# Three reorderings in a selective-scan kernel: the loads at its head, the spread of C behind dt, and attention steps beside the last slots of the layers

## The chip, the cores and the metric

The kernel runs on one core of a Trainium2 chip. The metric is device time in microseconds (us) of the whole program, lower is better. A core has a matrix engine (PE), a vector engine (DVE), an activation engine (ACT), a general engine (POOL) and a queue engine (SP) that in this kernel issues nearly all DMAs. Each of them runs its own list of instructions in the order of the program and waits on semaphores for the others.

## The reference, cut to what matters

The input `x` is two images of 128 channels and 64x64 pixels. Four layers follow. The first (`_L0`) is a 1x1 embedding, two blocks of a Mamba mixer and a feed-forward, and a 1x1 output with a residual. The mixer is where most of the first two thousand microseconds go:

```python
xz = x @ in_w.T; u, z = split(xz)                    # 128 -> 2 x 256 channels
u = silu(causal_conv(u, conv_w, 4 taps) + conv_b)
dt, Bm, Cm = split(u @ xproj_w.T, [8, 8 + 16])       # per pixel: 8, 16 and 16 numbers
dt = softplus(dt @ dt_w.T + dt_b)                    # 256 channels
dA = exp(dt[..., None] * A);  dBu = (dt * u)[..., None] * Bm[:, :, None, :]
h = dA_t * h + dBu_t;  y_t = einsum('bdn,bn->bd', h, C_t)     # over 4096 pixels
y = (y + u * ssm_D) * silu(z);  return y @ out_w.T
```

The second layer (`_L1`) has queries, keys and values from 3x3 convolutions, softmax attention over all 4096 pixels and a residual. The third (`_L2`) is the same with 1x1 convolutions. The fourth (`_L3`) has convolutions at four scales and a small attention between them. The change touches the first layer and its border with the second.

## The kernel before

**Items and slots.** An item is one chunk of 512 pixels of one block of one image: `items` has 2 images x 2 blocks x 8 chunks = 32 of them. The 256 channels times 16 states of an item are scanned in 8 groups of 32 channels; a group is four scans, each of 128 partitions (32 channels x 4 states) by 512 pixels. So an item has 32 slots of one scan. The body of a slot is `slot(i, todo, t_)`, run for i from -2 to 31 and then for a tail. `background(i)` writes by hand which pieces of the neighbouring items go into which slot (`at(slot, function, ...)`): for the next item n = i+1 the mixer's front, for i-1 and i-2 the mixer's back and the feed-forward, for i+2 the embedding and the layer norm. The schedule is manual: every engine gets its instructions in just this order.

**One item.** `pu_taps` (PE) makes u with the conv folded into the weights `wu`; `pu_out` (ACT) adds the bias; `silu` runs in slot 11; `xproj` in slot 13 and `xproj_out` in slot 14 give dt, B and C. `spread_bc` then stores B and C to a DRAM tile `dr` (1 DMA) and reads them back broadcast over the partitions: B into `bb` with four DMAs of 256 KB, C into `cb` with four more. `soft_plus` (slot 17) and `dt_end` (POOL, slot 18) give dt and dt*u. For each group, `spread_dt` copies dt of 32 channels four times into `dtb` (four DMAs of 64 KB, ring of four buffers, three groups ahead), `spread_dtu` brings dt*u onto 128 partitions with a matmul (`pdu`), `times_b` multiplies it with B into `h` on DVE, `decay` makes `da` = exp(dt*A) on ACT, `scan` runs the recurrence on DVE, and when a group's four scans are done POOL multiplies `h` with C. `y_pair` sums on PE. `ln_centre` to `ln_shift` are the layer norm.

**The head.** SP issues first the constants, then all eight chunks of image 0, then the embedding's weights `we`, then for each of the two blocks `wl`, `cw` (conv taps and the u half of the weights), `wd`, then the raw 3x3 weights `raw` (3 loads) and image 1. DVE multiplies `wu` from `cw`, and a short chain ACT, DVE, PE, DVE makes `am` (A spread over the partitions), for both blocks, before slot 0 of i = -2. In the slots of i = -1, `fold(k)` for k = 0, 1, 2 turns the raw weights into the form the attention's convolutions want (10 DVE operations) and stores them to DRAM as `ufold` (2 DMAs): in slots 2, 10 and 18.

**The tail.** The scans end with i = 31. The slots of i = 32 and 33 finish the last items' mixer and feed-forward (gelu in slot 3, `ffn_down` in slots 6 and 7, `ffn_add` in 9, `out_mm` in 11, `out_add` in 12 of the last round). Beside them a generator `beginning()` makes the first queries and the keys of the attention: `inputs` (12 DVE operations on the image, in two parts of 8 and 4), `products_by` (six groups of matmuls, with a `yield` after each), `outputs` (2 ACT and 9 DVE operations). The digits of

```python
beside = '2111001000112111111011010000'
```

say how many `next(steps)` stand in front of each tail slot, from slot 8 on; what remains runs after the last slot. The generator has 31 yields: 1 for the start, 6 for the queries, 6 for each of four chunks of keys (cc = 0 to 3). After that come the attention's scores, evicted by DVE (`sc`).

Of the kernel before, what the change touches and what calls it, by code (L numbers as in the profile page):

```python
# [6 lines left out]
F32 = mybir.dt.float32  # L7
AF = mybir.ActivationFunctionType
ALU = mybir.AluOpType
# [4 lines left out]
B, C, H, W = 2, 128, 64, 64  # L14
N = H * W
P = 128
CH = 512
NCH = N // CH
RPC = CH // W
NL = 2  # L20
DS = 16
DI = 2 * C
NJ = DI // P
R = (C + 15) // 16
NX = R + 2 * DS
KC = 4
# [41 lines left out]
def tile_conv_seq(ctx: ExitStack, tc, x, consts, vecs, wemb, wlay, wconv, wdt, wqkv, wsmall, wms, out):  # L68
    nc = tc.nc
# [9 lines left out]
    def xv(b, c):  # L79

        return xt[:, b, 1 + c * RPC : 1 + (c + 1) * RPC, 1 : W + 1]
# [7 lines left out]
        nc.gpsimd.memset(xt[:, b, 1 : H + 1, 0:1], 0.0)  # L89
        nc.gpsimd.memset(xt[:, b, 1 : H + 1, W + 1 : W + 2], 0.0)  # L90

    for c in range(NCH):
        nc.sync.dma_start(xv(0, c), x[0, :, c * RPC : (c + 1) * RPC, :])

    ud = ctx.enter_context(tc.tile_pool(name="ufold", bufs=1, space=bass.MemoryType.DRAM))
    ufold = [ud.tile([P, 18, C], F32, name=f"ufold{k}") for k in range(3)]
# [17 lines left out]
    with tc.manual_schedule(), ExitStack() as s:  # L114
# [22 lines left out]
            return fsel[:, g].rearrange("p q d -> p (q d)")  # L137

        nc.scalar.preload_act_table_set(EXP_LN_SET)
        wl, wu, wd, am = [], [], [], []  # L140
        for l in range(NL):
            w = wp.tile([P, NWL - DI], F32, name=f"wl{l}")
            nc.sync.dma_start(w, wlay[l][:, DI:])
            cw = sp.tile([P, KC + 1, DI], F32, name="cw", tag="h", bufs=5)
            nc.sync.dma_start(cw[:, :KC, :].rearrange("p k d -> p (k d)"), wconv[l : l + 1, :].to_broadcast([P, KC * DI]))
            nc.sync.dma_start(cw[:, KC, :], wlay[l][:, :DI])
            d = wp.tile([R, DI], F32, name=f"wd{l}")
            nc.sync.dma_start(d, wdt[l])

            u = wp.tile([P, KC, DI], F32, name=f"wu{l}")  # L150
            for k in range(KC):
                nc.vector.tensor_tensor(u[:, k, :], cw[:, KC, :], cw[:, k, :], ALU.mult)
            an = wp.tile([P, NJ * DS], F32, name=f"an{l}")
            nc.scalar.activation(an, vec[:, VEC[f"A_log{l}"] : VEC[f"A_log{l}"] + NJ * DS], AF.Exp)
            nc.vector.tensor_scalar(an, an, -1.0, None, ALU.mult)
            a = wp.tile([P, NJ, 4, 4], F32, name=f"am{l}")
            for g in range(4):
                pa = mm.tile([P, NJ, DS], F32, name="pa", tag="mm")
                nc.tensor.matmul(pa.rearrange("p j n -> p (j n)"), lhsT=four(g), rhs=an, start=True, stop=True)
                for q in range(4):  # L160
                    at = slice(32 * q, 32 * q + 32)
                    nc.vector.tensor_copy(a[at, :, g, :], pa[at, :, 4 * q : 4 * q + 4])
            wl.append(w), wu.append(u), wd.append(d), am.append(a)
        raws = []
        for which in range(3):
            raw = sp.tile([P, 3, 3, C], F32, name="raw", tag="h", bufs=5)
            nc.sync.dma_start(raw.rearrange("p y x c -> p (y x) c"), wqkv[:, which])
            raws.append(raw)
        for c in range(NCH):
            nc.sync.dma_start(xv(1, c), x[1, :, c * RPC : (c + 1) * RPC, :])  # L170

        def fold(which):

# [150 lines left out]
            st[i]["dbl"] = sp.tile([NX, CH], F32, name="dbl", tag="dbl")  # L324
            nc.scalar.copy(st[i]["dbl"], st[i].pop("pd"))

        def spread_bc(i):

            dr = dp.tile([2 * DS, CH], F32, name="dr", tag="dr")
            nc.sync.dma_start(dr, st[i]["dbl"][R:])  # L330
            for k in range(2):
                o = st[i]["bc", k] = sp.tile([P, 4, CH], F32, name=("bb", "cb")[k], tag=("bb", "cb")[k], bufs=2)
                for q in range(4):
                    src = dr[k * DS + 4 * q : k * DS + 4 * q + 4, :].rearrange("(o m) f -> o (m f)", o=1)
                    nc.sync.dma_start(o[32 * q : 32 * q + 32].rearrange("p m f -> p (m f)"), src.to_broadcast([32, 4 * CH]))

        def dtproj(i, j):
            st[i]["pt", j] = mmt("pt")
# [131 lines left out]
        def background(i):  # L470

            todo = [[] for _ in range(NSL)]

            def at(t, f, *a):
                todo[t].append((f, a))

            n, p, q, r = i + 1, i - 1, i - 2, i + 2
            if has(q):
                at(3, gelu, q)
                at(6, ffn_down, q, (0, 1)), at(7, ffn_down, q, (2, 3)), at(9, ffn_add, q)  # L480
                at(11, out_mm, q), at(12, out_add, q)
            if has(p):
                at(7, y_out, p, 1), at(7, gate, p)
                at(9, mix_out, p), at(11, mix_add, p)
            if has(n):
                at(0, pu_taps, n, 0, (0, 1)), at(1, pu_taps, n, 0, (2, 3)), at(2, pu_out, n, 0)
                at(3, pu_taps, n, 1, (0, 1)), at(4, pu_taps, n, 1, (2, 3)), at(5, pu_out, n, 1)
                at(13, xproj, n), at(14, xproj_out, n), at(14, spread_bc, n)
                at(15, dtproj, n, 0), at(16, dtproj, n, 1), at(17, soft_plus, n), at(18, dt_end, n)
            if has(i):  # L490
                at(1, pz_mm, i, 0), at(3, pz_out, i, 0)
                at(5, pz_mm, i, 1), at(6, pz_out, i, 1)
            if has(i) or has(n):
                at(11, silu, i, n)
            if i == -1:
                for k in range(3):
                    at(8 * k + 2, fold, k)
            pair = [(k, second) for k, second in ((p, True), (r, False)) if has(k)]
            if has(r):
                at(10, embed, r), at(11, embed_out, r)  # L500
            w, m = {}, len(pair)
            for k, (it, second) in enumerate(pair):
                at(12 + 2 * k, ln_centre, w, k, it)
                at(13 + 2 * k, ln_square, w, k, it)
                at(27, ln_spread, w, k, m), at(28, ln_scale, w, k, it)
                at(29, ln_shift, w, k, it, second)
            if pair:
                at(17, ln_var, w, m), at(18, ln_eps, w, m), at(19, ln_rs, w, m), at(20, ln_newton, w, m), at(21, ln_step, w, m)
            if has(p):
                for f in range(4):  # L510
                    at(30 + f // 2, ffn_up, p, f)
            if has(i):
                at(24, y_out, i, 0)
            return todo
# [6 lines left out]
        def slot(i, todo, t_):  # L521
            t = i * NSL + t_
            g, m = divmod(t, 4)
            if m == 0 and 0 <= g + 3 < NG:
                spread_dt(g + 3)
            if m == 0 and 0 <= g + 1 < NG:
                spread_dtu(g + 1)
            if m == 0 and g % 2 == 1 and 0 <= g - 3 < NG:
                y_pair(g - 3)
            if 0 <= t < NT:  # L530
                scan(t)
            if 0 <= t + 4 < NT:
                decay(t + 4)
            if m == 3 and 0 <= g + 1 < NG:
                times_b(g + 1)
            for f, a in todo[t_]:
                f(*a)
# [305 lines left out]


        steps = beginning()
        beside = '2111001000112111111011010000'
        for k in range(8, 2 * NSL):
            if k == NSL:
                todo = background(NI + 1)
# [523 lines left out]
```

## Time and profile before

| | us |
|---|---|
| median of three runs (5076.55 to 5080.12) | 5076.93 |
| the profiled execution | 5077.7 |
| its span, first to last instruction | 5075.9 |
| first scan starts | 84.94 |
| last scans of the layers end | 2102.91 |
| last `out_add` of the layers starts | 2166.28 |
| first eviction of attention scores starts | 2189.13 |
| mean granted PE clock | 0.948 |

Busy over the span: PE 92%, DVE 81%, ACT 47%, POOL 46%. In the profile a line number is that of the kernel before. A line of the timeline gives the start in us, the duration in us, engine, line, operation, what it writes and reads, its shape, how many were merged, and in brackets how long the engine stood idle before it and what ended that idle time. SPq and ACTq are the issuing of a DMA, not its transfer.

### The profile page before, as it was taken

To read this page: it belongs to the slowest core of one execution; us is meant where nothing else is said; L and a number is where in the kernel's file an instruction comes from. 1 tells how busy PE (TensorE), PEld (TensorE's weight loads), DVE (VectorE), ACT (ScalarE), POOL (GpSimd) and SP (SyncE) were. 2 spreads that over 40 slices of the span, in tenths; PEclk is the share of its full clock that TensorE was granted. 3 is DMA by queue.
4 is the path that set the end of the run, shared out by engine and by line. 5 is a ranking of instruction groups with operands and counts; after the bars stand their busy time and mean duration, and the time that the engine had idled before them with its cause. 6 is when DMAs were issued, how large, how long until landed. Compare 5 with 4: busy or idle time off the path is not lost.

```text
span 5075.9 us, 48999 instructions
## 1 busy us (share of the span) xinstructions
PE 4683.8 (92%) x14797; PEld 2250.9 (44%) x14797; DVE 4097.5 (81%) x4416; ACT 2366.9 (47%) x3221; POOL 2316.3 (46%) x1948
## 2 busy tenths in 40 slices
PE   5889999999988899889999999999999999999997
PEld 1222222222222222356666666666666666333332
DVE  5999999999999999788888878667766775667775
ACT  4677777777777777522222222333333332323332
POOL 2777776766777777413332233233333332322331
PEclk8898889988999989899999999999999999999998
DMA  5333333333333333124443344444444443000000
GB/s 149 72 69 68 70 71 70 72 69 68 69 70 68 72 72 71 46 54 102 105 102 84 77 104 103 118 97 111 111 100 99 112 111 77 5 5 7 7 7 7
DMA packets 237016, 373.86 MB, mean 74 GB/s; under 512 B 88000, under 2 KB 88400, under 8 KB 228432
## 3 DMA queue, kind: packets, MB, share of 16 engines
q1 hardware_dynamic: 187600, 303.55, 25.8%
q10 hardware_dynamic: 49152, 67.17, 5.8%
q8 instruction: 118, 1.93, 0.2%
q14 instruction: 146, 1.20, 0.1%
HBM read 92.18 MB, written 9.83 MB: 20 GB/s over the span
## 4 chain that ended last, share of the span: by engine, by line
PE 47%; POOL 21%; DVE 13%; issue 11%; DMA 3%; ACT 3%; SPq 2%; ACTq 0%; DVEq 0%; POOLq 0%
POOL h L391 16%; PE po L775 13%; PE pq L725 13%; DVE tr L755 3%; DMA pt<-tr 2%; PE pf L1060 2%; SPq L766 2%; PE py L403 2%; PE pqkv L1087 2%; PE pu L292 1%; PE pw L1146 1%; POOL dtu L351 1%; PE pfus L1211 1%; POOL z L414 1%; PE psc L1111 1%
## 5 line engine op out<-in xcount | busy, mean ns | idle before, releaser
L762 POOL COPY pt<-tr 32x512 f32<-32x512 f32 x1024 | 656.1, 641 | 1468.2 <-DVE tr L755 738.8
L388 DVE TENSOR_TENSOR_SCAN h<-da,carry,h 128x512 f32<-128x512 f32 x1024 | 1241.4, 1266 | 60.4 <-ACT da L377 31.6
L391 POOL TENSOR_TENSOR h<-h,cb 128x2048 f32<-128x2048 f32 x256 | 1161.1, 4536 | 20.8 <-POOL carry L390 0.2
L725 PE MATMUL pq<-k,q 128*128 128x512 f32 x2048 | 965.1, 594 | 11.2 <-DVE sc L730 8.8
L775 PE MATMUL po<-pt,vt 128*128 128x256 f32 x4096 | 967.5, 380 | 2.4 <-DMA pt<-tr 2.4
L740 ACT ACTIVATE sc<-sc,nm 128x2048 f32<-128x2048 f32 x256 | 510.6, 1995 | 937.2 <-DVE nm L736 641.7
L730 DVE TENSOR_SCALAR_CACHE_REDUCE sc<-pq 128x1024 f32<-128x1024 f32 x512 | 624.9, 1222 | 359.8 <-PE pq L725 337.9
L775 PEld LDWEIGHTS po<-pt,vt 128*128 128x128 f32 x4096 | 780.5, 191 | 293.9 <-issue 211.1
L377 ACT ACTIVATE da<-dtb,am 128x512 f32<-128x512 f32 x1024 | 681.7, 684 | 222.1 <-DVE h L388 210.6
L755 DVE STREAM_TRANSPOSE tr<-sc 128x2048 f32<-128x2048 f32 x256 | 591.6, 2311 | 65.8 <-DMA pt<-tr 60.5
L370 DVE TENSOR_TENSOR h<-bb,pdu 128x2048 f32<-128x2048 f32 x256 | 581.7, 2272 | 77.4 <-PE py L403 29.3
L403 PE MATMUL py<-h,sel 128*32 128x512 f32 x2048 | 511.5, 643 | 1.6 <-POOL h L391 1.6
L725 PEld LDWEIGHTS pq<-k,q 128*128 128x128 f32 x2048 | 384.5, 191 | 289.5 <-issue 247.1
L364 PE MATMUL pdu<-dtu,fsel 128*128 128x512 f32 x512 | 326.5, 724 | 101.9 <-DVE h L370 101.8
L403 PEld LDWEIGHTS py<-h,sel 128*32 128x32 f32 x2048 | 115.7, 118 | 415.9 <-issue 408.9
L292 PE MATMUL pu<-xn,wu 128*128 128x512 f32 x512 | 246.2, 615 | 3.0 <-ACT xn L282 2.1
L364 PEld LDWEIGHTS pdu<-dtu,fsel 128*128 128x128 f32 x512 | 96.2, 215 | 308.3 <-DVE h L370 187.6
L390 POOL COPY carry<-h 128x4 f32<-128x4 f32 x256 | 47.5, 185 | 388.1 <-DVE h L388 383.5
L1153 DVE TENSOR_TENSOR ov<-v,pw 128x2048 f32<-128x2048 f32 x64 | 146.2, 2285 | 68.5 <-PE pw L1146 68.5
L1087 PE MATMUL pqkv<-f,ws 128*128 128x512 f32 x384 | 189.7, 619 | 3.0 <-DVE prod L1104 2.3
L1157 POOL TENSOR_TENSOR ov<-ov 128x2048 f32<-128x2048 f32 x16 | 72.6, 4537 | 257.6 <-DVE ov L1153 257.6
L351 POOL TENSOR_TENSOR dtu<-dt,u 128x1024 f32<-128x1024 f32 x32 | 75.0, 2345 | 189.7 <-ACT dt L345 189.7
(241 smaller groups left out, 5344.1 us busy)
## 6 DMA issues: line engine op xcount, KB each, us to landing
pt<-tr SPq DMA_DIRECT2D x2048, 64.0 KB, 2.0
dtb<-dt SPq DMA_DIRECT2D x1024, 64.0 KB, 2.0
pt<-tr ACTq DMA_DIRECT2D x1024, 64.0 KB, 2.2
bb<-dr SPq DMA_DIRECT2D x128, 256.0 KB, 4.6
cb<-dr SPq DMA_DIRECT2D x128, 256.0 KB, 7.6
uw<-ufold SPq DMA_DIRECT2D x14, 576.0 KB, 3.7
xt<-in_x SPq DMA_DIRECT2D x16, 256.0 KB, 5.0
xr<-in_x SPq DMA_DIRECT2D x16, 256.0 KB, 2.9
```

The costliest lines, as they stand in the source:

```text
L364: nc.tensor.matmul(pdu, lhsT=four(s_ % 4), rhs=st[i]["dtu"][:, s_ // 4, :], start=True, stop=True)
L370: nc.vector.tensor_tensor(h, st[i]["bc", 0], pdu.unsqueeze(1).to_broadcast([P, 4, CH]), ALU.mult)
L377: nc.scalar.activation(da, st[i]["dtb", s_], AF.Exp, scale=am[items[i][1]][:, j, gg, m : m + 1])
L388: nc.vector.tensor_tensor_scan(h[:, m, :], da, h[:, m, :], carries[b, l][:, j, gg, m : m + 1], ALU.mult, ALU.add)
L391: nc.gpsimd.tensor_tensor(h, h, st[i]["bc", 1], ALU.mult)
L403: nc.tensor.matmul(py[r : r + 32, :], lhsT=sel, rhs=st[i]["h", s_ + k][:, m, :], start=(m == 0), stop=(m == 3), tile_position=(0, r),)
L725: nc.tensor.matmul(pq[:, i, :], lhsT=sta["q", r, grp][:, it * P : (it + 1) * P], rhs=sta["k"][:, at : at + CH], start=True, stop=True)
L730: nc.vector.tensor_scalar(dst, pq, 1.0, None, ALU.mult, ALU.max, accum_out=sta["mx"][:, c2 : c2 + 1])
L740: nc.scalar.activation(sc, sc, AF.Exp, bias=nm, scale=scale, accum_out=sm[:, hh : hh + 1])
L755: nc.vector.transpose(tr, sta.pop(("sc", r, blk, hh)).rearrange("p (t r f) -> p r t f", r=NB, f=32))
L762: nc.gpsimd.tensor_copy(dst, src)
L775: nc.tensor.matmul(sta["po", r, grp], lhsT=sta["vt"][:, jt, :], rhs=rhs, start=(jt == 0), stop=(jt == N // P - 1))
```

## The change

There are three parts.

1. **Head.** `we`, chunk 0 of image 0 and block 0's `cw`, `wl`, `wd` are issued first, then chunk 1, the other six chunks and block 1's weights. The loads of the raw weights and of image 1 are issued from slot 1 of i = -1. Making `am` and `wu` is a function `prepare(l)`, in which `am` now comes first and `wu` second; block 0's stands before the slots as before, block 1's moves to slot 7 of i = -1. The three folds move from slots 2, 10, 18 to slots 8, 9, 10. The first group's `spread_dtu` and `times_b` move from slots 28 and 31 of i = -1 to slots 19 and 26.
2. **B and C.** `spread_bc` gets an argument k: B (with the store of `dr`) stays in slot 14, C moves to slot 22. The DMAs of `spread_dt` in slots 16 and 20 so stand in front of C's four in SP's order.
3. **Tail.** `beside` keeps its first 24 digits; the four zeros after them become eleven ones. So eleven more steps stand beside slots 0 to 10 of the last round, and 2 instead of 13 remain after it.

```diff
--- before.py
+++ after.py
@@ -89,8 +89,8 @@
         nc.gpsimd.memset(xt[:, b, 1 : H + 1, 0:1], 0.0)
         nc.gpsimd.memset(xt[:, b, 1 : H + 1, W + 1 : W + 2], 0.0)
 
-    for c in range(NCH):
-        nc.sync.dma_start(xv(0, c), x[0, :, c * RPC : (c + 1) * RPC, :])
+    def load_x(b, c):
+        nc.sync.dma_start(xv(b, c), x[b, :, c * RPC : (c + 1) * RPC, :])
 
     ud = ctx.enter_context(tc.tile_pool(name="ufold", bufs=1, space=bass.MemoryType.DRAM))
     ufold = [ud.tile([P, 18, C], F32, name=f"ufold{k}") for k in range(3)]
@@ -137,19 +137,21 @@
             return fsel[:, g].rearrange("p q d -> p (q d)")
 
         nc.scalar.preload_act_table_set(EXP_LN_SET)
-        wl, wu, wd, am = [], [], [], []
-        for l in range(NL):
+        load_x(0, 0)
+        wl, wu, wd, am, cws = [], [], [], [], []
+
+        def load_layer(l):
+            cw = sp.tile([P, KC + 1, DI], F32, name="cw", tag="h", bufs=5)
+            nc.sync.dma_start(cw[:, KC, :], wlay[l][:, :DI])
+            nc.sync.dma_start(cw[:, :KC, :].rearrange("p k d -> p (k d)"), wconv[l : l + 1, :].to_broadcast([P, KC * DI]))
+            cws.append(cw)
             w = wp.tile([P, NWL - DI], F32, name=f"wl{l}")
             nc.sync.dma_start(w, wlay[l][:, DI:])
-            cw = sp.tile([P, KC + 1, DI], F32, name="cw", tag="h", bufs=5)
-            nc.sync.dma_start(cw[:, :KC, :].rearrange("p k d -> p (k d)"), wconv[l : l + 1, :].to_broadcast([P, KC * DI]))
-            nc.sync.dma_start(cw[:, KC, :], wlay[l][:, :DI])
             d = wp.tile([R, DI], F32, name=f"wd{l}")
             nc.sync.dma_start(d, wdt[l])
-
-            u = wp.tile([P, KC, DI], F32, name=f"wu{l}")
-            for k in range(KC):
-                nc.vector.tensor_tensor(u[:, k, :], cw[:, KC, :], cw[:, k, :], ALU.mult)
+            wl.append(w), wd.append(d)
+
+        def prepare(l):
             an = wp.tile([P, NJ * DS], F32, name=f"an{l}")
             nc.scalar.activation(an, vec[:, VEC[f"A_log{l}"] : VEC[f"A_log{l}"] + NJ * DS], AF.Exp)
             nc.vector.tensor_scalar(an, an, -1.0, None, ALU.mult)
@@ -160,14 +162,28 @@
                 for q in range(4):
                     at = slice(32 * q, 32 * q + 32)
                     nc.vector.tensor_copy(a[at, :, g, :], pa[at, :, 4 * q : 4 * q + 4])
-            wl.append(w), wu.append(u), wd.append(d), am.append(a)
+
+            u, cw = wp.tile([P, KC, DI], F32, name=f"wu{l}"), cws[l]
+            for k in range(KC):
+                nc.vector.tensor_tensor(u[:, k, :], cw[:, KC, :], cw[:, k, :], ALU.mult)
+            wu.append(u), am.append(a)
+
         raws = []
-        for which in range(3):
-            raw = sp.tile([P, 3, 3, C], F32, name="raw", tag="h", bufs=5)
-            nc.sync.dma_start(raw.rearrange("p y x c -> p (y x) c"), wqkv[:, which])
-            raws.append(raw)
-        for c in range(NCH):
-            nc.sync.dma_start(xv(1, c), x[1, :, c * RPC : (c + 1) * RPC, :])
+
+        def load_rest():
+            for which in range(3):
+                raw = sp.tile([P, 3, 3, C], F32, name="raw", tag="h", bufs=5)
+                nc.sync.dma_start(raw.rearrange("p y x c -> p (y x) c"), wqkv[:, which])
+                raws.append(raw)
+            for c in range(NCH):
+                load_x(1, c)
+
+        load_layer(0)
+        load_x(0, 1)
+        prepare(0)
+        for c in range(2, NCH):
+            load_x(0, c)
+        load_layer(1)
 
         def fold(which):
 
@@ -324,15 +340,16 @@
             st[i]["dbl"] = sp.tile([NX, CH], F32, name="dbl", tag="dbl")
             nc.scalar.copy(st[i]["dbl"], st[i].pop("pd"))
 
-        def spread_bc(i):
-
-            dr = dp.tile([2 * DS, CH], F32, name="dr", tag="dr")
-            nc.sync.dma_start(dr, st[i]["dbl"][R:])
-            for k in range(2):
-                o = st[i]["bc", k] = sp.tile([P, 4, CH], F32, name=("bb", "cb")[k], tag=("bb", "cb")[k], bufs=2)
-                for q in range(4):
-                    src = dr[k * DS + 4 * q : k * DS + 4 * q + 4, :].rearrange("(o m) f -> o (m f)", o=1)
-                    nc.sync.dma_start(o[32 * q : 32 * q + 32].rearrange("p m f -> p (m f)"), src.to_broadcast([32, 4 * CH]))
+        def spread_bc(i, k):
+
+            if k == 0:
+                st[i]["dr"] = dp.tile([2 * DS, CH], F32, name="dr", tag="dr")
+                nc.sync.dma_start(st[i]["dr"], st[i]["dbl"][R:])
+            dr = st[i]["dr"]
+            o = st[i]["bc", k] = sp.tile([P, 4, CH], F32, name=("bb", "cb")[k], tag=("bb", "cb")[k], bufs=2)
+            for q in range(4):
+                src = dr[k * DS + 4 * q : k * DS + 4 * q + 4, :].rearrange("(o m) f -> o (m f)", o=1)
+                nc.sync.dma_start(o[32 * q : 32 * q + 32].rearrange("p m f -> p (m f)"), src.to_broadcast([32, 4 * CH]))
 
         def dtproj(i, j):
             st[i]["pt", j] = mmt("pt")
@@ -485,7 +502,7 @@
             if has(n):
                 at(0, pu_taps, n, 0, (0, 1)), at(1, pu_taps, n, 0, (2, 3)), at(2, pu_out, n, 0)
                 at(3, pu_taps, n, 1, (0, 1)), at(4, pu_taps, n, 1, (2, 3)), at(5, pu_out, n, 1)
-                at(13, xproj, n), at(14, xproj_out, n), at(14, spread_bc, n)
+                at(13, xproj, n), at(14, xproj_out, n), at(14, spread_bc, n, 0), at(22, spread_bc, n, 1)
                 at(15, dtproj, n, 0), at(16, dtproj, n, 1), at(17, soft_plus, n), at(18, dt_end, n)
             if has(i):
                 at(1, pz_mm, i, 0), at(3, pz_out, i, 0)
@@ -493,8 +510,10 @@
             if has(i) or has(n):
                 at(11, silu, i, n)
             if i == -1:
+                at(1, load_rest), at(7, prepare, 1)
                 for k in range(3):
-                    at(8 * k + 2, fold, k)
+                    at(8 + k, fold, k)
+                at(19, spread_dtu, 0), at(26, times_b, 0)
             pair = [(k, second) for k, second in ((p, True), (r, False)) if has(k)]
             if has(r):
                 at(10, embed, r), at(11, embed_out, r)
@@ -523,7 +542,7 @@
             g, m = divmod(t, 4)
             if m == 0 and 0 <= g + 3 < NG:
                 spread_dt(g + 3)
-            if m == 0 and 0 <= g + 1 < NG:
+            if m == 0 and 1 <= g + 1 < NG:
                 spread_dtu(g + 1)
             if m == 0 and g % 2 == 1 and 0 <= g - 3 < NG:
                 y_pair(g - 3)
@@ -531,7 +550,7 @@
                 scan(t)
             if 0 <= t + 4 < NT:
                 decay(t + 4)
-            if m == 3 and 0 <= g + 1 < NG:
+            if m == 3 and 1 <= g + 1 < NG:
                 times_b(g + 1)
             for f, a in todo[t_]:
                 f(*a)
@@ -843,7 +862,7 @@
 
 
         steps = beginning()
-        beside = '2111001000112111111011010000'
+        beside = '21110010001121111110110111111111111'
         for k in range(8, 2 * NSL):
             if k == NSL:
                 todo = background(NI + 1)
```

## The prediction

> **What bounds the kernel now.** I read the page first, then the timeline of its two borders. In the page's slices of 127 us DVE is busy nine tenths from the second to the fifteenth, so the layers between 127 and about 2000 us are DVE's: whatever the change takes from other engines there is worth nothing unless DVE waits for it. The first slice is different:
>
> ```profile
> PE   5889999999988899889999999999999999999997
> DVE  5999999999999999788888878667766775667775
> ```
>
> So the head and the border (near 2100 to 2190 us, slices 17 and 18) are where time can go. DVE's timeline of the head shows why:
>
> ```profile
> 19.58 1.43 DVE L152 TENSOR_TENSOR wu<-cw 128x256 f32<-128x256 f32 x4 [15.18 <-DMA cw<-in_wlay]
> 20.93 0.17 DVE L155 TENSOR_SCALAR an<-an 128x32 f32<-128x32 f32 x1
> 21.83 2.89 DVE L162 COPY am<-pa 32x8 f32<-32x8 f32 x16 [0.73 <-PE pa L159]
> ...
> 45.09 0.75 DVE L269 SCALAR_TENSOR_TENSOR cen<-cen,vec,pr 128x512 f32<-128x512 f32 x1 [15.16 <-PE pr L265]
> ...
> 79.44 0.75 DVE L269 SCALAR_TENSOR_TENSOR cen<-cen,vec,pr 128x512 f32<-128x512 f32 x1 [18.42 <-PE pr L265]
> 81.45 2.29 DVE L370 TENSOR_TENSOR h<-bb,pdu 128x2048 f32<-128x2048 f32 x1 [1.26 <-DMA ufold<-ulo]
> 84.94 4.81 DVE L388 TENSOR_TENSOR_SCAN h<-da,carry,h 128x512 f32<-128x512 f32 x4 [1.20 <-ACT da L377]
> ```
>
> DVE stands idle 15 us for the first `cw`, which lies behind 2 MB of image in the queue, then for the layer norm, then for B, dt and item 1's norm. From 84.94 us on it runs without a gap. SP's timeline shows what stood in front of dt:
>
> ```profile
> 67.04 0.32 SPq L330 DMA_DIRECT2D dr<-dbl  x1
> 68.65 1.71 SPq L335 DMA_DIRECT2D bb<-dr  x4
> 70.41 1.81 SPq L335 DMA_DIRECT2D cb<-dr  x4
> 72.31 0.37 SPq L188 DMA_DIRECT2D ufold<-ulo  x1
> 73.30 0.34 SPq L188 DMA_DIRECT2D ufold<-uhi  x1
> 74.45 16.03 SPq L359 DMA_DIRECT2D dtb<-dt  x19
> ```
>
> 1 MB of B, 1 MB of C and 1.2 MB of the third fold go out before the first dt, and over 70 to 83 us the 16 DMA engines move 264 GB/s with no idle share. At the border DVE waits for ACT, whose `df` stands behind the layers' last `out_add`:
>
> ```profile
> 2166.28 0.69 ACT L467 ACTIVATE xt<-po,vec 128x512 f32<-128x512 f32 x1 [2.13 <-PE po L463]
> 2166.86 0.47 ACT L571 ACTIVATE df<-pa,vec 128x256 f32<-128x256 f32 x1
> ```
> ```profile
> 2167.62 0.42 DVE L640 TENSOR_TENSOR k<-df,pa 128x256 f32<-128x256 f32 x1 [15.93 <-ACT df L639]
> ```
>
> [...] So order of issue is order of arrival, near enough. The trace agrees: the first dt, issued at 74.45 us behind 3.2 MB, lands 8.8 us later, where 2.0 us is the median of dt's DMAs. [...] The image's rows are such pieces, and the trace has 233 GB/s while they load (2 to 12 us) against 377 for mostly weights (14 to 26 us). [...]
>
> **Head, step by step.** *Loads.* In front of block 0's `cw` there will be constants, `we`, one chunk of image: with `cw` 1.4 MB instead of 4 MB. The first image chunk took 4.5 us from issue to landing and is issued near 2.1 us behind `we`: about 7 us. `cw` (640 KB, at an estimated 330 GB/s between the two rates above) then lands near 9. `am` no longer waits for it: `fsel` ends at 4.39, and from `an` to the end of `am` was 3.8 us, so DVE has `am` at 8.1 and PE its last `pa` at 7.4. The embedding's matmul, first at 29.31, follows `pa` as it did before: 7.5. Block 1's `prepare`, 5.2 us of DVE in front of it, is gone from here. So embedding, norm and `pu` shift by 21.8 us: `pu` from 46.74 to 24.9, its end (9.9 us) to 34.8. `wu` (1.4 us) is ready near 10.5, covered by the norm's 15 us.
>
> *Given back.* In slot 7 of i = -1 block 1's `an` stands on ACT behind `pu_out`, so at 35.6. `prepare(1)` then takes DVE 5.2 us (0.17 + gaps + 2.89 + 1.43) to 41.0. Only then come the folds, three times 5.1 us (45.76 to 61.02 before): they end at 56.3. Before, they ran beside `pu`. On SP the six `ufold` DMAs (slots 8 to 10) now precede `dr` (slot 14), and SP waits in order. `dbl` is ready at 46.8 (66.44 + 0.59 - 21.8, and 1.5 for PE's `prepare` matmuls in front of the embedding), but `dr` goes out at 56.7, ten us later. This is the new wait: **SP stands on the third fold**. PE, ACT and POOL lose nothing by it; their `pd`, `dt` (49.6), `dtu` (52), `pdu` (54) come under those ten us.
>
> *From dr to the scan.* `dr` landed 1.6 us after issue before; with 0.6 MB of `ufold` in front I take 2.9: `bb` from 59.65, four issues, all landed 6.2 us later (68.65 to 74.85 before): 65.8. dt follows at once: issued 61.4 to 63.8, landed about 66 behind B. `times_b` (slot 26) 65.9 to 68.2, item 1's `cen` (slot 28) to 68.9, `da` at 66.8. First scan **68.9 instead of 84.94: -16.0 us**. C is issued after dt at 63.8, 1 MB lands by 71.5, and POOL wants it at 73.9; the second dt lands near 72.7, wanted by ACT at about 73. Both fit by about 1 to 2 us. After that the state is the old one, shifted.
>
> **C behind dt, 31 times.** Before, C stood in front of the dt of slot 16. ACT's wait for it is small:
>
> ```profile
> ACT da L377 <- DMA dtb<-dt: 0.3, 1, 0.3
> ```
>
> That is all from 127 to 2100 us, so the gain is at most 1 us: I take 0. The price: C is issued behind dt of slots 16 and 20. Near 305 us B goes out at 305.89, and dt of slot 20 waits for soft plus (309.56), so C moves from 307.68 to about 312. C's longest landing is 9.8 us: 322. Its first reader is POOL at 339.23. Slack 17 us; cost 0. If that cover were gone, POOL's product would be late, then `y_pair`, then an `h` buffer and DVE.
>
> **Tail.** Durations from the rows of before, with PE in order. Step 20 used to start on DVE with 8 of `inputs` at 2147.26 to 2151.7, the same now. Its two `df` follow ACT's last `hid` (2153.88) instead of `out_add` (2166.97): 13.0 us earlier. DVE's `outputs` 2154.6 to 2158.6, the last 4 `inputs` to 2161.2, the next 8 to 2165.6, `outputs` of cc 2 to 2169.4, 4 `inputs` to 2172.0. PE: four `pa` groups of cc 2 (5.3 us) from 2153.2; two `pb` wait for `dhi`, 2160 to 2162.8; first `pa` of cc 3 to 2164.4. **`ffn_down` stands behind these**: it began at 2157.15, now at 2164.4, the added wait. Behind it are `ffn_add`, `out_mm`, `out_add` and the last `df`. In a busy PE its 10 matmuls cost 4.3 us (3.59 for 8 near 2059) instead of 6.3. With two more `pa` groups (2.7) and a third (1.35) and a `pb` (1.35): 2174.1. `out_mm` 1.8 to 2175.9, `out_add` to 2176.6, `df` 0.7, DVE's last `outputs` 4.0: the first score eviction at **2181.3 instead of 2189.13: -7.8 us**. DVE alone would give -13; 5 us go back to PE's order. The scores were already there before DVE came to them (`pq` began at 2186.42) and are again (2177). Everything after shifts.
>
> **Sum.** -16.0 + 0 - 7.8 = -23.8 on the profiled 5077.7 (span 5075.9 and 1.8 around it): 5053.9. The median of the runs shown is 0.8 under the profiled one: **5053 us**.
>
> **Rivals.** *More* (0.14): SP is not what decides, so the scan starts when DVE is free of the folds: 56.3 + 2.3 + 0.7 = 59.4, -25.5; with the tail -33, 5044. Against it: SP's order in the diff. For it: `ufold` is small if queued early. *Less* (0.20): the loads' gain is smaller [...] (image chunk and `cw` land 4 us later), B and dt take 3 us more behind `ufold`, C's first product or the second dt stalls the second group, [...]: -11 to -16, 5061 to 5066. *The loads gain nothing* (0.04): if transfers interleaved rather than queued, `cw` and the first chunk would land near 19 as now; the scan then starts later than 80 and the sum is -7 or less. The dt row above speaks against. *Slower* (0.05): C comes too late in the steady state. It decides if C is issued over 17 us after where I put it, past 329 near item 3. Were SP held so long by dt's ring of four, DVE would wait; at 2 us beyond the point, 31 items x 2 = 62, so +38: 5115. Against: ring waits on SP are at most 10.0 us.
>
> **Numbers.** My case has 0.57. A measurement tells about 0.2%, 10 us, from no change. Faster by more than that: 0.57 + 0.14 + 0.20 = 0.91; within 0.04; slower 0.05. Range: the unknowns are the landing of `dr`, B and dt behind `ufold` (-13 to -20 for the head), PE's clock at the border (-4 to -11) and 2 us of spread between runs. With the rival "more" below and most of "less" above: 5041 to 5066.
>
> **What would show it.** Right: embedding near 7.5, third fold's end near 56, `dr` on SP just behind it, first scan near 69, the gap between first and last scan unchanged (2018 us within 5), `pf` at the border delayed behind `pa`/`pb` against `hid`, first eviction some 24 us earlier than 2189. Wrong: `dr` near 47 (SP not held); a POOL wait for `cb` in each item; DVE's first group followed by a gap; a first eviction less than 13 us earlier.

## The result, and the profile after

| | median us | range | runs |
|---|---|---|---|
| before | 5078.58 | 5076.55 to 5080.68 | 5 |
| changed | 5056.2 | 5054.5 to 5058.0 | 5 |

The ratio is 0.9956, with a 95% interval of 0.9942 to 0.9971: 22 us faster. The profiled execution of the changed kernel has a span of 5055.7 us, where before had 5075.9; the granted PE clock is 0.947 against 0.948. In what follows a span is cut into four stages: up to the start of the first scan, from there to the end of the last scan, from there to the first eviction of scores (the border), and the rest.

| us, from the profiles | first scan | to last scan's end | border | rest |
|---|---|---|---|---|
| before | 84.94 | 2017.97 | 86.22 | 2886.8 |
| changed | 72.65 | 2018.20 | 78.16 | 2886.7 |

The head gave 12.3 us, the border 8.1, the rest nothing. The page's slices of the changed kernel show no more than that the first one is fuller, on both engines by a tenth:

```profile
PE   6889999999888998889999999999999999999997
DVE  6999999999999999788888877667766775667775
```

DVE's timeline of the head says where it stands now (line numbers are those of the changed kernel: L157 and L164 make `am`, L168 `wu`, L193 to L202 are the fold, L285 the norm's product, L387 `times_b`, L405 the scan):

```profile
9.58 1.43 DVE L168 TENSOR_TENSOR wu<-cw 128x256 f32<-128x256 f32 x4 [1.28 <-DMA cw<-in_wconv]
23.46 0.75 DVE L285 SCALAR_TENSOR_TENSOR cen<-cen,vec,pr 128x512 f32<-128x512 f32 x1 [12.45 <-PE pr L281]
35.53 0.18 DVE L157 TENSOR_SCALAR an<-an 128x32 f32<-128x32 f32 x1 [11.32 <-ACT an L156]
...
50.65 2.50 DVE L193 TENSOR_TENSOR ulo<-raw 128x384 f32<-128x384 f32 x1
...
54.65 1.61 DVE L197 SCALAR_TENSOR_TENSOR uhi<-raw 128x384 f32<-128x384 f32 x1
...
56.69 1.66 DVE L199 SCALAR_TENSOR_TENSOR ulo<-raw,uhi 128x384 f32<-128x384 f32 x1
...
69.79 2.29 DVE L387 TENSOR_TENSOR h<-bb,pdu 128x2048 f32<-128x2048 f32 x1 [9.93 <-DMA bb<-dr]
72.00 0.74 DVE L285 SCALAR_TENSOR_TENSOR cen<-cen,vec,pr 128x512 f32<-128x512 f32 x1
72.65 4.80 DVE L405 TENSOR_TENSOR_SCAN h<-da,carry,h 128x512 f32<-128x512 f32 x4
```

The wait for the first `cw` is down from 15.18 us to 1.28, the first norm comes 21.6 us earlier, and then a wait of 9.93 us for B stands at the end, behind a long third fold. SP's timeline, at the place that was shown of before:

```profile
58.38 0.32 SPq L204 DMA_DIRECT2D ufold<-ulo  x1
59.89 0.32 SPq L204 DMA_DIRECT2D ufold<-uhi  x1
60.30 0.40 SPq L347 DMA_DIRECT2D dr<-dbl  x1
62.97 1.71 SPq L352 DMA_DIRECT2D bb<-dr  x4
64.78 2.50 SPq L376 DMA_DIRECT2D dtb<-dt  x4
67.32 2.71 SPq L352 DMA_DIRECT2D cb<-dr  x4
```

`dr` follows the third fold's last store by 0.4 us, though `dbl` was ready at 47.56. dt now goes in front of C. At the border, PE first, then ACT, then DVE:

```profile
2147.80 2.86 PE L641 MATMUL pb<-dhi,uw 128*128 128x256 f32 x12 [1.52 <-DVE dhi L627]
2150.86 1.53 PE L641 MATMUL pa<-uw 128*128 128x256 f32 x6 [0.20 <-DVE uw L620]
2152.23 1.88 PE L465 MATMUL pf<-hid,wl 128*128 128x512 f32 x4
```
```profile
2163.68 0.69 ACT L484 ACTIVATE xt<-po,vec 128x512 f32<-128x512 f32 x1 [4.97 <-PE po L480]
2164.26 0.47 ACT L590 ACTIVATE df<-pa,vec 128x256 f32<-128x256 f32 x1
```
```profile
2165.03 0.42 DVE L659 TENSOR_TENSOR k<-df,pa 128x256 f32<-128x256 f32 x1 [5.15 <-ACT df L658]
```

ACT's `df` still stands behind the layers' last `out_add`, but DVE waits 5.15 us for it instead of 15.93, and only the last chunk of keys is left to do. The price is on PE: `pf`, the feed-forward's second half, whose gelu had ended at 2145.7, starts at 2152.23, behind `pa` and `pb`.

### The profile page after: what moved, and what is told of

Same layout as the page of the kernel before. It is cut to its first block, busy times and chain, and to the rows that moved or that the text cites. A ratio compares the mean times of both kernels' runs of the same rounds, so it can differ in the third digit from the quotient of the medians.

```text
span 5055.7 us, 49003 instructions
## 1 busy us (share of the span) xinstructions
PE 4678.3 (93%) x14797; PEld 2245.1 (44%) x14797; DVE 4102.2 (81%) x4416; ACT 2366.8 (47%) x3221; POOL 2316.9 (46%) x1948
## 4 chain that ended last, share of the span: by engine, by line
PE 48%; POOL 21%; DVE 13%; issue 11%; ACT 3%; DMA 2%; SPq 2%; ACTq 0%; DVEq 0%; POOLq 0%
POOL h L408 17%; PE po L794 14%; PE pq L744 14%; DVE tr L774 3%; PE pf L1079 2%; PE pqkv L1106 2%; PE py L420 2%; DMA pt<-tr 2%; SPq L785 2%; PE pw L1165 1%; POOL dtu L368 1%; POOL z L431 1%; PE pfus L1230 1%; DVE h L405 1%; PE pu L308 1%
## 5 line engine op out<-in xcount | busy, mean ns | idle before, releaser
L405 DVE TENSOR_TENSOR_SCAN h<-da,carry,h 128x512 f32<-128x512 f32 x1024 | 1241.6, 1266 | 59.4 <-ACT da L394 30.7
L744 PE MATMUL pq<-k,q 128*128 128x512 f32 x2048 | 965.4, 594 | 11.1 <-DVE sc L749 8.8
L387 DVE TENSOR_TENSOR h<-bb,pdu 128x2048 f32<-128x2048 f32 x256 | 581.8, 2273 | 85.9 <-PE py L420 29.2
```

Source lines behind the costliest of these rows:

```text
L387: nc.vector.tensor_tensor(h, st[i]["bc", 0], pdu.unsqueeze(1).to_broadcast([P, 4, CH]), ALU.mult)
L405: nc.vector.tensor_tensor_scan(h[:, m, :], da, h[:, m, :], carries[b, l][:, j, gg, m : m + 1], ALU.mult, ALU.add)
L744: nc.tensor.matmul(pq[:, i, :], lhsT=sta["q", r, grp][:, it * P : (it + 1) * P], rhs=sta["k"][:, at : at + CH], start=True, stop=True)
```

## The experiments

The theory: three parts add up. The head gains by block 1's preparation leaving the front, and gives part back where SP stands on the third fold; C's place matters only in the head; the border gains until PE's order binds. Each run is read from its own profile first, by stages: the rest behind the border, which no edit touches, takes between 2883.6 and 2888.7 us in the twelve profiles, so a gain of 4 us can be seen in its stage and still be lost in the time. The head, too, differs by 1 to 2 us between profiles (see the end).

| us | first scan | to last scan's end | border | median | ratio to before (95%) |
|---|---|---|---|---|---|
| no_tail | 71.60 | 2018.05 | 86.32 | 5063.78 | 0.9974 (0.9964 to 0.9984) |
| tail_only | 83.19 | 2017.28 | 78.05 | 5068.45 | 0.9979 (0.9971 to 0.9987) |
| c_back | 77.08 | 2017.95 | 78.06 | 5061.8 | 0.9969 (0.9957 to 0.9981) |
| c_only | 82.84 | 2018.05 | 86.31 | 5074.74 | 0.9994 (0.9986 to 1.0003) |
| store_late | 64.01 | 2017.31 | 78.16 | 5048.86 | 0.9945 (0.9930 to 0.9960) |
| pool_off | 68.79 | 2018.97 | 78.16 | 5054.29 | 0.9955 (0.9941 to 0.9968) |
| loads_only | 82.34 | 2016.97 | 87.00 | 5075.59 | 0.9996 (0.9988 to 1.0004) |
| early | 58.45 | 2019.66 | 78.16 | 5044.59 | 0.9935 (0.9923 to 0.9948) |
| tail_string | 72.38 | 2017.95 | 74.43 | 5053.39 | 0.9956 (0.9941 to 0.9971) |
| early_tail | 58.96 | 2016.45 | 74.46 | 5040.37 | 0.9930 (0.9918 to 0.9943) |

**Do the parts add up?** The change without its tail, and the tail alone:

```diff
--- changed
-        beside = '21110010001121111110110111111111111'
+        beside = '2111001000112111111011010000'
```

> The change without its tail part (the old string of digits beside the tail's slots). Theory: the three parts add up and don't touch each other. First scan at 72.65 us as in the whole change, 2018 us from the first scan to the last, and from the end of the last scan to the first eviction of scores 86.2 us as before: about 12 us faster than before, 5066. Rival (the parts lean on each other: what the head wins is lost again later unless the tail goes with it): within 4 us of before.

```diff
--- before
-        beside = '2111001000112111111011010000'
+        beside = '21110010001121111110110111111111111'
```

> Before with only the eleven more steps beside the tail's slots. Theory: first scan at 84.9 us, the border 78.2 us instead of 86.2 from the end of the last scan to the first eviction, 8 us faster in all: about 5070. Rival (DVE alone sets the border): 13 us faster there. Second rival (the added wait of the feed-forward behind the products eats it): 3 us or less.

Both as the theory had it, and each leaves the other's stage alone: borders of 86.32 and 78.05 us, where before has 86.22 and the whole change 78.16. In time the two are 0.26% and 0.21% below before, together 0.47%; the whole change is 0.44%. So no part leans on another, the feed-forward's added wait does not eat the gain, and DVE alone does not set the border.

**Does C's place matter, and where?** C back behind B in the changed kernel, and C moved alone in the kernel before (there with the split `spread_bc` of the change):

```diff
--- changed
-at(14, spread_bc, n, 0), at(22, spread_bc, n, 1)
+at(14, spread_bc, n, 0), at(14, spread_bc, n, 1)
```

> The whole change with C's four DMAs back in slot 14, straight behind B's. Theory: it matters only in the head, where dt again lands behind 1 MB of C: the first scan 3 to 4.5 us later (near 76.5), 2018 us from the first scan to the last unchanged, about 5060. Rival (dt in front of C wins a little in each of 31 items): 10 to 30 us slower than the whole change, with a longer way from the first scan to the last. Second rival (C's place is of no account anywhere): first scan at 72.7.

```diff
--- before
-at(14, spread_bc, n)
+at(14, spread_bc, n, 0), at(22, spread_bc, n, 1)
```

> Before with only C's DMAs moved from slot 14 to slot 22. Theory: in the head the matmul pdu and then B set the start (81.45 us), so the first scan comes about 1 us earlier (83.8) and nothing changes in the items: 1 us faster, not to be told from no change. Rival (dt in front of C wins in each item): 10 to 30 us faster. Third (C now comes too late for POOL): slower, with POOL waiting for cb.

In c_back the first scan is 4.4 us later, and the way to the last scan is the same. ACT's and DVE's timelines name the wait, and the list of ACT's waits over all items (127 to 2090 us) shows that the items lose next to nothing:

```profile
77.08 4.81 DVE L405 TENSOR_TENSOR_SCAN h<-da,carry,h 128x512 f32<-128x512 f32 x4 [3.73 <-ACT da L394]
```
```profile
76.30 1.30 ACT L394 ACTIVATE da<-dtb,am 128x512 f32<-128x512 f32 x2 [19.34 <-DMA dtb<-dt]
```
```profile
ACT da L394 <- DMA dtb<-dt: 6.2, 4, 2.9
```

ACT stands 6.2 us in four waits, DVE's scans none the longer for it. c_only cannot be told from before in time; its first scan, 2.1 us earlier, is within 0.4 us of tail_only, which has before's head unchanged. Its timelines say why so little comes of it:

```profile
78.25 1.30 ACT L378 ACTIVATE da<-dtb,am 128x512 f32<-128x512 f32 x2 [3.32 <-DMA dtb<-dt]
```
```profile
78.42 0.75 DVE L269 SCALAR_TENSOR_TENSOR cen<-cen,vec,pr 128x512 f32<-128x512 f32 x1 [17.92 <-PE pr L265]
80.42 2.29 DVE L371 TENSOR_TENSOR h<-bb,pdu 128x2048 f32<-128x2048 f32 x1 [1.26 <-DMA cb<-dr]
82.84 4.81 DVE L389 TENSOR_TENSOR_SCAN h<-da,carry,h 128x512 f32<-128x512 f32 x4
```

dt came 6 us earlier, and ACT made `da` at 78.25 instead of 84.16. But item 1's norm and B's product behind it set DVE's start (the bracket at B's product names a DMA, but what ended just ahead of it is PE's `pdu`, at 80.38), and the scan's own wait for `da` had been only 1.20 us. Nearly all of that went; the other 1 us is the norm's earlier place in this profile. So dt in front of C is worth 4 us in the changed head, where B's product and the norm come earlier, about 1 us in the old head, and nothing in the items. That C would come too late shows in no run.

**Is it the order of the loads?** The loads in the new order, all else as before:

```diff
--- before
-    for c in range(NCH):
-        nc.sync.dma_start(xv(0, c), x[0, :, c * RPC : (c + 1) * RPC, :])
...
+        load_x(0, 0)
         wl, wu, wd, am = [], [], [], []
         for l in range(NL):
-            w = wp.tile([P, NWL - DI], F32, name=f"wl{l}")
-            nc.sync.dma_start(w, wlay[l][:, DI:])
...
             nc.sync.dma_start(cw[:, KC, :], wlay[l][:, :DI])
+            w = wp.tile([P, NWL - DI], F32, name=f"wl{l}")
+            nc.sync.dma_start(w, wlay[l][:, DI:])
...
             nc.sync.dma_start(d, wdt[l])
+            for c in (range(1, NCH) if l == 0 else ()):
+                load_x(0, c)
```

> Before with only the order of the loads changed (embedding weights, first chunk, block 0's cw first); both blocks are still prepared before the slots, folds, C and the tail stay as before. Theory (the shift by 21.8 us comes from taking block 1's preparation out of the front as much as from the order): the embedding's first matmul now waits for block 1's cw, 27 us instead of 29.3, first scan near 83, about 2 us faster: 5075.5. Rival (the order of the loads alone makes the gain of the head): embedding near 8, first scan at 73 or earlier, 5065.

PE's timeline has block 1's `pa` waiting for an `an` that stands behind block 1's `cw`, and the embedding behind it:

```profile
24.52 1.03 PE L162 MATMUL pa<-an,fsel 128*128 128x32 f32 x4 [10.41 <-DVE an L158]
...
27.43 2.05 PE L220 MATMUL pe<-xt,we 128*128 128x512 f32 x2
```

The embedding at 27.43 us, as the theory's 27; in the changed kernel it is at 7.68. The time cannot be told from before. Without moving block 1's preparation out of the front, the order of the loads gains nothing that can be told from the spread. The reverse, the preparation moved and the loads as before, was not run; that the new order is needed rests on the old head alone, where DVE waited for block 0's `cw` until 19.58 us. Nor was `am` ahead of `wu`, or the first `times_b` in slot 26 instead of 31, run alone: what each gives lies within the 12.3 us.

**Does SP stand on the third fold?** Its two stores go behind the first dt and C, DVE's work unchanged:

```diff
--- changed, in fold and in background
-            for k, u in enumerate((lo, hi)):
-                nc.sync.dma_start(ufold[which][:, 9 * k : 9 * k + 9, :], u.rearrange("p s y c -> p (s y) c"))
+            def store():
+                for k, u in enumerate((lo, hi)):
+                    nc.sync.dma_start(ufold[which][:, 9 * k : 9 * k + 9, :], u.rearrange("p s y c -> p (s y) c"))
+            stores.append(store)
+            if which < 2:
+                store()
...
-                at(19, spread_dtu, 0), at(26, times_b, 0)
+                at(19, spread_dtu, 0), at(29, lambda: stores[2]()), at(26, times_b, 0)
```

> The whole change with the two stores of the third fold moved in SP's order from slot 10 to slot 29, behind the first dt and C. DVE's work is the same. Theory (SP stands on the third fold): dr goes out behind the second fold's stores, at 51 us instead of 60.3, B has landed near 60.5, first scan at 63.4 instead of 72.65, the way to the last scan unchanged: 9 us faster than the whole change, about 5047. Rival (DVE's own 20 us of prepare and folds set the start, SP only follows them): the first scan moves by less than 3 us.

```profile
51.32 0.32 SPq L207 DMA_DIRECT2D ufold<-uhi  x1
51.73 0.41 SPq L353 DMA_DIRECT2D dr<-dbl  x1
54.34 1.71 SPq L358 DMA_DIRECT2D bb<-dr  x4
```

`dr` goes out behind the second fold, and the first scan starts at 64.01, 8.6 us earlier than in the changed kernel, with the third fold on DVE as long as there. SP's order it was; DVE's 20 us are not what set the start. They are close behind, though: the fold ends at 60.38 in this run, and B's product starts at 61.14, with B landed only 0.8 us after DVE was free.

**Why is the third fold long?** Three of its operations took 2.50, 1.61 and 1.66 us. POOL's timeline of the changed kernel has three operations that end at 52.74, 55.85 and 57.93, each 0.4 us ahead of the end of one of the three:

```profile
50.40 2.34 POOL L368 TENSOR_TENSOR dtu<-dt,u 128x1024 f32<-128x1024 f32 x1 [29.06 <-ACT dt L362]
54.50 1.35 POOL L272 TENSOR_TENSOR nt<-nt,ve 1x512 f32<-1x512 f32 x1 [1.76 <-ACT nt L267]
56.68 1.25 POOL L277 TENSOR_TENSOR rs<-rs,nt 1x512 f32<-1x512 f32 x1 [0.83 <-ACT nt L273]
```

So I gave them to DVE in that round alone (`now_i[0]` holds the round):

```diff
--- changed, in dt_end, ln_newton and ln_step
-            nc.gpsimd.tensor_tensor(w["dtu"], w["dt"], w["u"], ALU.mult)
+            (nc.vector if i == 0 else nc.gpsimd).tensor_tensor(w["dtu"], w["dt"], w["u"], ALU.mult)
...
-            nc.gpsimd.tensor_tensor(nt, nt, w["ve"][:n], ALU.mult)
+            (nc.vector if now_i[0] == -1 else nc.gpsimd).tensor_tensor(nt, nt, w["ve"][:n], ALU.mult)
...
-            nc.gpsimd.tensor_tensor(rs, rs, w["nt"][:n], ALU.mult)
+            (nc.vector if now_i[0] == -1 else nc.gpsimd).tensor_tensor(rs, rs, w["nt"][:n], ALU.mult)
```

> The whole change with the three POOL operations of round i = -1 (dt*u, and the two small products of the layer norm) on DVE. DVE gets about 2 us more to do. Theory (three DVE operations of the third fold, 2.50, 1.61 and 1.66 us instead of about 0.56, stood still until a POOL operation ended): the third fold takes 5.1 us instead of 9.2, dr goes out near 56.1 instead of 60.3, first scan near 68.6, about 4 us faster than the whole change: 5052. Rival (they waited for a buffer that a store had yet to free, not for POOL): the three stay long, nothing gained. Second rival (the added DVE work delays B's product as much): first scan within 1 us of 72.65.

```profile
50.90 0.55 DVE L193 TENSOR_TENSOR ulo<-raw 128x384 f32<-128x384 f32 x1
...
52.94 0.55 DVE L197 SCALAR_TENSOR_TENSOR uhi<-raw 128x384 f32<-128x384 f32 x1
...
53.92 0.56 DVE L199 SCALAR_TENSOR_TENSOR ulo<-raw,uhi 128x384 f32<-128x384 f32 x1
```

All three are short; the fold takes 5.1 us, `dr` goes out at 56.44 and the first scan starts at 68.79, 3.9 us earlier, as forecast for POOL and against a wait for buffers, which this edit does not touch. In the timed runs the ratio (0.9955) cannot be told from the whole change's (0.9956): the verdict is the profile's.

**Versions that beat both.** If SP stands on folds, the folds belong where DVE is idle and SP has nothing urgent. `load_layer` is cut in two, `load_cw` and `load_wl`:

```diff
--- changed
-        load_layer(0)
-        load_x(0, 1)
-        prepare(0)
-        for c in range(2, NCH):
-            load_x(0, c)
-        load_layer(1)
+        load_cw(0)
+        for which in range(3):
+            raw = sp.tile([P, 3, 3, C], F32, name="raw", tag="h", bufs=5)
+            nc.sync.dma_start(raw.rearrange("p y x c -> p (y x) c"), wqkv[:, which])
+            raws.append(raw)
+        load_wl(0)
+        load_x(0, 1)
+        prepare(0)
+        for c in range(2, NCH):
+            load_x(0, c)
...
+            if i == -2:
+                at(14, fold, 0), at(30, fold, 1), at(31, fold, 2)
             if i == -1:
-                at(1, load_rest), at(7, prepare, 1)
-                for k in range(3):
-                    at(8 + k, fold, k)
+                at(6, load_cw, 1), at(7, prepare, 1)
+            if 0 <= i < NCH:
+                at(9, load_x, 1, i)
+            if i == 0:
+                at(9, load_wl, 1)
```

> The whole change with the raw weights loaded straight behind block 0's cw, the folds in slots 14, 30 and 31 of i = -2 (beside the layer norm and pu), block 1's cw in slot 6 of i = -1, its other weights and image 1 in the slots of the first items. Theory (SP stands on the folds, and they are slowed by POOL only where they meet it): dr goes out as soon as dbl is there, near 48 us; B has landed at 55.5; then the layer norm of item 1 sets the start: its product on DVE ends at 60.8, first scan 60.8 instead of 72.65, 12 us faster than the whole change, about 5044. Rival (the loads moved in between hold SP or the DMA engines as long): first scan later than 70. Second rival (image 1's chunks, one per item, disturb dt in the items): a longer way from the first scan to the last than 2018 us.

```profile
33.88 0.32 SPq L202 DMA_DIRECT2D ufold<-uhi  x1
...
45.37 0.33 SPq L345 DMA_DIRECT2D dr<-dbl  x1
46.99 1.72 SPq L350 DMA_DIRECT2D bb<-dr  x4
```
```profile
54.02 2.29 DVE L385 TENSOR_TENSOR h<-bb,pdu 128x2048 f32<-128x2048 f32 x1 [13.23 <-DMA bb<-dr]
57.79 0.75 DVE L283 SCALAR_TENSOR_TENSOR cen<-cen,vec,pr 128x512 f32<-128x512 f32 x1 [1.48 <-PE pr L279]
58.45 4.80 DVE L403 TENSOR_TENSOR_SCAN h<-da,carry,h 128x512 f32<-128x512 f32 x4
```

`dr` goes out 0.02 us after `dbl` is there (44.77 + 0.58), SP having had nothing to issue since block 1's `cw` at 34.76; what ends last ahead of the first scan is the norm of item 1, as expected, though 2.4 us earlier than expected. The start is 14.2 us earlier than the changed kernel's. The items take 1.5 us more in this profile, but early_tail, with the same loads among them, takes 1.8 less than the changed kernel: a disturbance by them is not shown.

The border's other five microseconds were put down to PE's order. The digits that let the feed-forward pass (seven steps instead of eleven beside the last round, so four more run after it):

```diff
--- changed
-        beside = '21110010001121111110110111111111111'
+        beside = '211100100011211111101101111100003'
```

> The whole change with other digits from slot 0 of the last round on: '111100003' instead of '11111111111', so that the feed-forward's second half stands on PE ahead of the third chunk's last two groups, and five more steps run after the last slot. Theory (of the 13 us that DVE alone would give at the border, 5 went to PE's order, where ffn_down stood behind products that wait for DVE): ffn_down starts at about 2146 instead of 2152, the last two conversions come after the last products instead of after the last out_add, the border takes 74.2 us instead of 78.2: about 4 us faster than the whole change, 5052. Rival (DVE's chain of inputs and outputs sets the border): within 1 us of 78.2.

```profile
2145.58 3.60 PE L465 MATMUL pf<-hid,wl 128*128 128x512 f32 x8
2149.01 1.02 PE L467 MATMUL pf<-xt,kc 128*128 128x512 f32 x2
2149.88 2.75 PE L641 MATMUL pb<-dhi,uw 128*128 128x256 f32 x12
```
```profile
2160.33 0.42 DVE L659 TENSOR_TENSOR k<-df,pa 128x256 f32<-128x256 f32 x1 [0.98 <-ACT df L658]
```

`pf` starts at 2145.58, ahead of `pb`; DVE's last wait for `df` is 0.98 us instead of 5.15, and the border is 74.43 us instead of 78.16. In time alone the run cannot be told from the whole change (0.9956 both).

Both edits together, `early`'s and these digits:

> Both: the early folds of 'early' and the digits of 'tail_string'. Theory: the shares add up; first scan near 58.5, about 2019.5 us to the last, border 74.2: about 4 us faster than 'early' and 16 faster than the whole change, 5040.5. Rival (they share a cause): no faster than 'early'.

5040.37 us, 0.9930 of before (0.9918 to 0.9943), with both shares in their stages. It has the lowest median of all, but in time it cannot be told from `early` (0.9935). Against the changed kernel, the profiled span is 17.1 us shorter and the median 15.8 us lower; each against the runs of before that go with it, 12.1 us (34.5 and 22.4).

## Why the prediction was right

It said 5053 us and the median is 5056.2. The waits it named are the ones that the runs show; one term of the head was too small. Its steps:

- *Loads.* Embedding forecast at 7.5 us, measured 7.68; `wu` ready 10.5, measured 11.0; `pu` at 24.9, measured 25.11. loads_only shows that the step was right to count block 1's preparation and not the order alone. The dt row is not the only one in which SP's transfers landed in the order of their issue: in the profile of before, block 0's `wl` and two parts of `cw` and block 1's three, issued at 11.15, 11.62, 12.10, 13.16, 14.11 and 14.73 us, landed at 17.0, 19.0, 19.5, 21.5, 22.8 and 23.1, and of the transfers issued from 69.48 us on, B's third landed at 74.4, C's first three at 76.8 to 79.2, the third fold's two at 81.6 and 83.0, and the first dt at 83.3. The image's rows are 256 bytes (64 numbers of 4 bytes): 8078 of the 8184 packets from 2 to 12 us (233 GB/s) are under 512 bytes, and 789 of the 1893 from 14 to 26 us (377 GB/s). That the size makes the difference of the rates was not shown.
- *Given back.* SP standing on the third fold was named ahead, and store_late shows it. The term that was mis-sized is "the folds, three times 5.1 us (45.76 to 61.02 before): they end at 56.3". They ended at 59.86. The third took 9.2 us (50.65 to 59.86), since I moved durations of a time when POOL was idle (from 43 to 61 us of before no POOL operation runs) to one in which it has three operations, and costed the fold as if only DVE were concerned. In the changed kernel's trace the three DVE operations that started while a POOL operation ran ended 0.4 us behind its end, and with POOL's work gone (pool_off) none was long (0.55 to 0.56 us). The profile of before had a hint, which I did not read: an `inputs` operation of 2.85 us at 2112.72 instead of 0.67, beside POOL's gate product (2112.30 to 2115.03).
- *From dr to the scan.* `dr` took 2.67 us (forecast 2.9), B 6.8 us from its first issue to DVE's product (forecast 6.2: the 74.85 us for B's landing before is no reading but the last issue, 69.94, plus 4.9, the longest landing shown; here the last of B's four took 5.4). With the fold's 3.6 us the first scan came at 72.65 instead of 68.9: -12.3 us, not -16.0.
- *C behind dt.* Forecast 0 in the items; the way from first to last scan changed by 0.2 us, and c_back and c_only agree. In the head it is worth 4.4 us (c_back), which the sum held in its landing times. The second dt did not fit, as the prediction had it, by 1 to 2 us: ACT stood 2.20 us for it, until 76.88, but DVE was still at the first group's scans.
- *Border.* Forecast -7.8, measured -8.1, with `ffn_down` behind the products as said (forecast 11.2 us behind the start of ACT's last `hid`, 2153.19 to 2164.4 in the old times; measured 11.1, 2141.14 to 2152.23). "DVE alone would give -13; 5 us go back to PE's order": tail_string got 3.7 of them. The working took the operations of ACT, DVE and PE as kept in the order of the program, and the profiles have it so: the `df` that starts at 2166.86 in before, right behind `out_add`, had no product of its `pa` to wait for after 2144.65, and `pf` in the changed kernel starts 6.5 us after its gelu's end. The shorter `pf` of the working came too: its 8 large matmuls took 5.40 us in before, behind 4.00 us without work, and 3.60 in tail_string, behind none. The mean granted PE clock was 0.98 over before's border and 0.99 over the changed one.
- *Sum.* -20.4 us by stages against -23.8 forecast; the spans differ by 20.2, the medians by 22.4. That the medians come nearer to the forecast than the stages is spread between runs, and luck; the stages are the better test.
- *A slip of reading.* DVE's row of slices has its nines from the second to the sixteenth slice, not the fifteenth; nothing rests on it.

The rival "more" fell because SP does decide; "less" had the right sign but other reasons (C and the second dt came in time for DVE: no gap above 0.1 us follows the first group). That the loads gain nothing fell with the embedding at 7.68 us. The slower rival, C too late, did not occur.

## What to carry to other kernels

Ask of every operation that is moved not only which engine it occupies but which queue then stands in order behind it: here two stores that nobody was waiting for cost 8.6 us, because a small and urgent transfer was next in SP's list. Take a duration along with an operation only if the other engines do the same beside it as they did where it was measured: here ten DVE operations that took 5.1 us beside an idle POOL took 9.2 with three of POOL's beside them. Where two chains share PE or ACT at a border, try the order by hand: here the same 31 steps took 86, 78 and 74 us, by their places alone.

## What the runs showed of the hardware that was not expected

- In the changed kernel's third fold, three DVE operations on two SBUF inputs that started while a POOL operation ran took 2.50, 1.61 and 1.66 us instead of 0.56 and ended 0.4 us after POOL's end. Beside them POOL took 2.34 us on 128 partitions, and 1.35 and 1.25 us on one partition. This is not only so in the head: in the same trace, thirteen of the 22 operations of L619 (`uw`, two SBUF inputs) start beside a POOL operation and take 1.09 to 2.86 us; the other nine take at most 0.69.
- The scans and `times_b` show nothing of the kind there. Of the 1024 scans, the 733 that start while POOL works and the 291 that don't have the same median, 1.26 us, and `times_b` stays within 2.26 to 2.29 us in both cases. Each has one of its two large inputs (`da`, `pdu`) in PSUM; that this is the reason was not shown.
- The same head varies from one profile to the next. Before and tail_only have one head, and the first scan is at 84.94 and 83.19; the 16 matmuls of the first `pu` took 9.90 us in the one and 8.77 in the other, and 9.55 and 8.89 in the changed kernel and no_tail. No run here tests the cause. It means that a head's gain below about 2 us is not read from one profile.
